# A selective-scan kernel: softplus's last sums moved from matmuls to VectorE for three of four images, and the spread of B issued earlier

## Chip, cores and metric

The kernel runs on one core of one Trainium2 chip. The metric is the device time of one execution in microseconds (us); lower is better. All arithmetic is fp32.

## What is computed

The input is four images of 48 x 48 pixels with 128 channels. Layer 0 is a state-space block with four scan directions; layer 1 is an attention over the pixels followed by a spectral convolution. Cut to what matters here (b image, k direction, d one of 256 inner channels, n one of 16 states, l position):

```python
x_dbl = jnp.einsum('bkdl,kcd->bkcl', xs, x_proj_w)
dts_r, Bs, Cs = x_dbl[:, :, :R], x_dbl[:, :, R:R + N], x_dbl[:, :, R + N:]
dts = jnp.einsum('bkrl,kdr->bkdl', dts_r, dt_proj_w)
dt = jax.nn.softplus(dts + dt_proj_b[None, :, :, None])
A = -jnp.exp(A_logs).reshape(K, d, N)
...
h = h * exp(dt_l * A) + (dt_l * u_l) * B_l      # scanned over l
y = sum over n of h * C_l
...
t = t + attention(layernorm(t))
t = t + spectral_convolution(layernorm(t))
```

The change is in how `dt = softplus(...)` is put together, and in where the spread of B stands in the order of the instructions.

## The kernel before, in words

**Stages.** The images go one after another. For each image there is a prologue (group norm, projections, depthwise convolution), the scans, an epilogue and the attention. The prologue of the next image is woven into the epilogue and the attention of this one. The spectral convolution of image b-1 (`tail`, then `stu`) is woven into the scans of image b; image 0's scans are woven with `mixture`, which makes the convolution's weights G out of the matrices M that it loads. The convolution of the last image runs alone at the end. In the trace the scans of image 0 lie from about 116 to 1202 us, those of images 1, 2 and 3 from about 1470 to 2883, 3149 to 4579 and 4847 to 6256 us.

**Scans.** An image has 24 chunks: four directions of six chunks of 384 positions (`CS`). A chunk has 8 units, one for each half h of the 256 channels and each quarter q of the states. A unit works on a tile s of 128 x 1536. L439 enters it (dt*x times B): on VectorE with B read from PSUM, or, for the three units in `POOLED`, (0, 3), (1, 1) and (1, 3), on GpSimd with B from a tile bc in SBUF. ScalarE makes dA = exp(A*dt) in four pieces (L444), VectorE scans the four pieces (L447), GpSimd copies the carry (L455) and multiplies by C (L456), and TensorE sums over the states (L464). After four units VectorE adds the sum to y (L470).

**Spread of B.** For a unit that VectorE enters, `Unit.spread` (L431) is one matmul that copies B's rows (partitions 32 to 63 of xd) over 128 partitions into a PSUM tile. There is one such tile, so the spread for unit s+2 waits until VectorE has entered unit s+1.

**Preparation of a chunk.** `Chunk.prep` is a generator of 20 steps. Steps 1 to 3 make xd with the matmuls of L354; steps 4 to 7 multiply it with dt's weights, once for each half (L364, rows 0 to 8), and ScalarE takes the absolute value e and the relu of the product (L366, L367). Step 9 is e = exp(-e) and u = 1 + e (L373, L374); step 11 is l = ln(u) and u - 1 (L377, L378). Then softplus is relu + ln(u) with a correction for the rounding of u: e - (u - 1) + l + relu. Four matmuls with an identity (or its negative) for each half make this sum in PSUM (L395); ScalarE copies it to SBUF (L398), and VectorE multiplies it by x (L401). Those are steps 12 and 13 for half 0 and 14 and 15 for half 1. The two results go to DRAM (`store`, L383) and come back replicated as rep (`load`, L388): half 0's store is issued in step 15, half 1's store and half 0's load in step 17, half 1's load in step 19.

**Order of the work.** The order is written out by hand in `scans`; each engine runs its own queue in that order. `prepare` is called twice for each unit, in its middle and at its end, and takes a step of the next chunk in units 0 to 5 of a chunk and of the chunk after in units 4 to 7. So step 11 falls in the middle of a chunk's second unit, step 12 at its end, steps 13 and 14 in the middle and at the end of the third, step 15 in the middle of the fourth. dt's matmuls fall at the ends of the sixth and the seventh unit. `more` takes pieces of the woven work (on images 1 to 3: conv, L945, with its copies on ScalarE, L954, and additions on VectorE, L965; projection, L1003) until a share of all TensorE columns of the stage has been issued; `CHUNK_COLS` counts those of a chunk. Conv has two PSUM tiles. The transfers of rep, bc, tt (the convolution's filters) and G are all issued from SP's queue, in order.

Of the kernel before, what the change touches and what calls it, by code (L numbers as in the profile page):

```python
# [9 lines left out]
AF = mybir.ActivationFunctionType  # L10
ALU = mybir.AluOpType
# [9 lines left out]
NH = D // P  # L21
CS = 384
# [32 lines left out]
def hybrid_kernel(ctx: ExitStack, tc: tile.TileContext, a: dict, out: bass.AP):  # L55
# [3 lines left out]
    nc = tc.nc  # L59
# [60 lines left out]
    spread = wp.tile([64, Q4, C4, DL], F32, name="spread")  # L120
# [6 lines left out]
    mone = wp.tile([P, 1], F32, name="mone")  # L127
# [189 lines left out]
    def in_order(t, k, lo, n):  # L317

        if k % 2 == 0:
            return t[:, lo // W:(lo + n) // W, :]  # L320
        return t.rearrange("p h w -> p w h")[:, lo // H:(lo + n) // H, :]

    def mm_tile(name):
        return psm.tile([P, 512], F32, tag="mm", name=name)

    class Chunk:


        def __init__(self, b, k, c):
            self.b, self.k, self.lo = b, k, c * CS  # L330
            self.name = f"{b}_{k}_{c}"
            self.bc, self.rep = {}, []
            self.rev = k >= 2
            self.first = c == (NCH - 1 if self.rev else 0)
            self.last = c == (0 if self.rev else NCH - 1)

# [6 lines left out]
        def prep(self, pool):  # L343

            k, name, xc = self.k, self.name, xcs[self.b]
            yield
            xd = self.xd = pool.xd.tile([64, CS], F32, tag="xd", name=f"xd{name}")  # L350
            bcd = self.bcd = dram.tile([32, CS], F32, tag="bcd", name=f"bcd{name}")
            ps = mm_tile(f"xp{name}")
            for h in range(NH):
                nc.tensor.matmul(ps[:64, :CS], xw[:, h, k, :], in_order(xc[h], k, self.lo, CS),  # L354
                                 start=(h == 0), stop=(h == NH - 1))
            yield 2 * CS
            nc.scalar.activation(xd, ps[:64, :CS], AF.Identity, bias=onerow)
            yield

            u, l = [pool.one.tile([P, NH, CS], F32, tag=f"tmp{v}", name=f"{v}{name}") for v in "ul"]  # L360
            re = pool.one.tile([P, NH, 2, CS], F32, tag="re", name=f"re{name}")
            for h in range(NH):
                ps = mm_tile(f"dt{name}_{h}")
                nc.tensor.matmul(ps[:, :CS], dtw[:, k, h * P:(h + 1) * P], xd[:R + 1], start=True, stop=True)  # L364
                yield CS
                nc.scalar.activation(re[:, h, 1], ps[:, :CS], AF.Abs)  # L366
                nc.scalar.activation(re[:, h, 0], ps[:, :CS], AF.Relu)  # L367
                if h == 0:
                    nc.sync.dma_start(bcd, xd[32:64])
                yield  # L370
            e = re[:, :, 1]
            yield 0
            nc.scalar.activation(e, e, AF.Exp, scale=-1.0)  # L373
            nc.scalar.activation(u, e, AF.Identity, bias=1.0)  # L374
            yield
            yield 0
            nc.scalar.activation(l, u, AF.Ln)  # L377
            nc.scalar.activation(u, u, AF.Identity, bias=mone)  # L378
            d = dram.tile([NH, DL, 2, G4, CS], F32, tag="dtdu", name=f"dtdud{name}")

            def store(h):
                for g in range(G4):
                    nc.sync.dma_start(d[h, :, :, g], re[g * DL:(g + 1) * DL, h])  # L383

            def load(h):
                rep = pool.rep.tile([P, 2, G4, CS], F32, tag="rep", name=f"rep{name}_{h}")
                for c in range(C4):
                    nc.sync.dma_start(rep[c * DL:(c + 1) * DL], d[h])  # L388
                self.rep.append(rep)

            yield
            for h in range(NH):
                ps = mm_tile(f"sp{name}_{h}")
                for i, (w, t) in enumerate(((ident, e[:, h]), (nident, u[:, h]), (ident, l[:, h]), (ident, re[:, h, 0]))):
                    nc.tensor.matmul(ps[:, :CS], w, t, start=(i == 0), stop=(i == 3))  # L395
                yield 4 * CS

                nc.scalar.copy(re[:, h, 0], ps[:, :CS])  # L398
                x = in_order(xc[h], k, self.lo, CS)
                w = x.shape[2]  # L400
                nc.vector.tensor_tensor(re[:, h, 1].rearrange("p (r w) -> p r w", w=w),  # L401
                                        ps[:, :CS].rearrange("p (r w) -> p r w", w=w), x, ALU.mult)
                if h == 1:
                    store(0)
                yield
            yield 0
            store(1)
            load(0)
            yield
            yield 0  # L410
            load(1)
            yield
# [60 lines left out]
    POOLED = ((0, 3), (1, 1), (1, 3))  # L473
    order = [(k, c) for k in range(K) for c in (range(NCH) if k < 2 else reversed(range(NCH)))]
    quads = [(h, q) for h in range(NH) for q in range(Q4)]
# [1 line left out]
    EARLY = 4  # L477
    FETCHED = sorted({q for h, q in POOLED} | set(range(Q4, 2 * Q4)))

    CHUNK_COLS = (len(quads) - len(POOLED)) * CS + len(quads) * CS + 12 * CS  # L480

    def begin_scans(b, pool):

# [12 lines left out]
    def scans(b, chunks, preps, front, sp, back, work, work_cols):  # L496

        units = [Unit(ch, h, q) for ch in chunks for h, q in quads]
        total = len(chunks) * CHUNK_COLS + work_cols
        done = [0]  # L500

        def more(share):

            while done[0] < share * total:
                cols = next(work, None)
                if cols is None:
                    break
                done[0] += cols

        def enter(s):  # L510

            if s + 2 < len(units) and units[s + 2].pool:
                units[s + 2].enter(sp.s)
            if 0 <= s + 1 < len(units) and not units[s + 1].pool:
                units[s + 1].enter(sp.s)

        def spread(s):
            if s < len(units) and not units[s].pool:
                units[s].spread(back.psB)
                done[0] += CS  # L520

        def prepare(s):

            ci, j = divmod(s, len(quads))
            for c in [ci + 1] * (j <= TURN + 1) + [ci + 2] * (j >= TURN):
                if c < len(chunks):
                    done[0] += next(preps[c], None) or 0

        def refill(s, i):

            if 0 <= s < len(units) and s // len(quads) + 1 < len(chunks):
                u, nxt = units[s], chunks[s // len(quads) + 1]
                if u.h == NH - 1:
                    nxt.fetch(i + u.q, front)

        pending = []
        spread(0)
        enter(-2)
        enter(-1)
        spread(1)  # L540
        for s in range(len(units) + 2):
            real = s < len(units)
            if pending and real:
                pending.pop().add_y()
            enter(s)
            if real:
                units[s].scan(0, back.psa)
            if 1 <= s <= len(units):
                units[s - 1].times_c()
            if real:  # L550
                units[s].scan(1, back.psa)
            prepare(s)
            more((s + 0.5) / len(units))
            spread(s + 2)
            if real:
                units[s].scan(2, back.psa)
                units[s].scan(3, back.psa)
            if pending:
                pending.pop().add_y()
            refill(s - 3, Q4)  # L560
            if s + 1 < len(units) and units[s + 1].pool:
                refill(s + 1, 0)
            if s >= 2:
                units[s - 2].sum_c(back.psy)
                done[0] += CS
                if units[s - 2].q == Q4 - 1:
                    pending.append(units[s - 2])
            more((s + 1) / len(units))
            prepare(s)
        for u in pending:  # L570
            u.add_y()
        assert next(work, None) is None
# [522 lines left out]
    for b in range(B):  # L1095
        sp = Stage(tc, f"h{b}", "left", s=(6, SB))
        ps = Stage(tc, f"b{b}", "right", psa=(2, PSUM), psy=(1, PSUM), psB=(1, PSUM), psc=(2, PSUM), psp=(1, PSUM))
        if b == 0:
            mixed = Stage(tc, "m", "right", two=(2, SB))
            scans(b, *first, front, sp, ps, mixture(mixed, ps), MIX_COLS)  # L1100
            mixed.close()
        else:
            scans(b, *first, front, sp, ps, later(b - 1, held, ps), STU_COLS + TAIL_COLS_ALL)
# [93 lines left out]
```

## Time and profile before

| | us |
|---|---|
| median of 3 runs (lowest, highest) | 7273.59 (7267.72, 7281.86) |
| the profiled execution's own time | 7258.27 |
| its span, first to last instruction | 7256.5 |
| TensorE busy (matmuls) | 6418.8 (88%) |
| VectorE busy | 4834.2 (67%) |
| ScalarE busy | 3020.6 (42%) |
| GpSimd busy | 3809.3 (52%) |
| mean granted TensorE clock | 0.914 |

The shares are means over stages with different limits, so the table of stretches, which gives each engine's busy time between two points of the span, is what a reading rests on. An fp32 matmul stands in the trace as two records. "PEld" is TensorE's loading of weights, which overlaps matmuls. In a wait, "X <- Y" means that X's engine sat idle until Y was done. A few per cent of the matmul records can be missing.

### The profile page before, as it was taken

To read this page: it belongs to the slowest core of one execution; us is meant where nothing else is said; L and a number is where in the kernel's file an instruction comes from. 1 tells how busy PE (TensorE), PEld (TensorE's weight loads), DVE (VectorE), ACT (ScalarE), POOL (GpSimd) and SP (SyncE) were. 2 spreads that over 40 slices of the span, in tenths; PEclk is the share of its full clock that TensorE was granted. 3 is DMA by queue.
4 is the path that set the end of the run, shared out by engine and by line. 5 is a ranking of instruction groups with operands and counts; after the bars stand their busy time and mean duration, and the time that the engine had idled before them with its cause. 6 is when DMAs were issued, how large, how long until landed. Compare 5 with 4: busy or idle time off the path is not lost.

```text
span 7256.5 us, 80192 instructions
## 1 busy us (share of the span) xinstructions
PE 6418.8 (88%) x26904; PEld 3706.4 (51%) x26904; DVE 4834.2 (67%) x6045; ACT 3020.6 (42%) x5984; POOL 3809.3 (52%) x1775
## 2 busy tenths in 40 slices
PE   4777777978999998978999999887999999889999
PEld 1333334434555565534555556533455556647788
DVE  6889986377788876457778886547878887412111
ACT  3666663444444443344444543244444543231000
POOL 2888885056677765035667775215667776300000
PEclk7777777979999999889999999888999999889999
DMA  3555553056667675046667676125667677215545
GB/s 96 137 137 136 133 135 93 22 131 151 166 167 193 174 195 171 14 102 144 157 165 190 179 192 189 47 62 131 166 167 183 184 183 205 78 31 140 152 145 177
DMA packets 648926, 1019.18 MB, mean 140 GB/s; under 512 B 93849, under 2 KB 506649, under 8 KB 623778
## 3 DMA queue, kind: packets, MB, share of 16 engines
q1 hardware_dynamic: 642816, 1010.84, 53.9%
q8 instruction: 214, 3.51, 0.2%
q10 hardware_dynamic: 5698, 3.21, 0.2%
q14 instruction: 198, 1.62, 0.1%
HBM read 895.86 MB, written 117.84 MB: 140 GB/s over the span
## 4 chain that ended last, share of the span: by engine, by line
PE 63%; DVE 20%; DMA 8%; ACT 3%; POOL 2%; issue 2%; SPq 2%; DVEq 0%; ACTq 0%; POOLq 0%
PE cv L945 26%; DVE s L447 11%; PE pr L1003 7%; PE y L464 5%; PE sp L395 5%; DVE s L439 4%; PE s L695 4%; PE B L431 4%; PE o L686 3%; DMA tt<-fd 2%; DMA G<-gd 2%; PE op L632 2%; PE dt L364 2%; PE xp L354 2%; POOL s L456 1%
## 5 line engine op out<-in xcount | busy, mean ns | idle before, releaser
L456 POOL TENSOR_TENSOR s<-s,bc 128x1536 f32<-128x1536 f32 x768 | 2645.0, 3445 | 263.5 <-DVE s L447 187.2
L447 DVE TENSOR_TENSOR_SCAN s<-dA,carry,s 128x384 f32<-128x384 f32 x2560 | 2444.7, 1005 | 311.9 <-ACT dA L444 307.8
L444 ACT ACTIVATE dA<-rep,A 128x384 f32<-128x384 f32 x3072 | 1748.3, 584 | 951.5 <-DVE s L447 935.4
L945 PE MATMUL cv<-tt,u 128*128 128x256 f32 (+4 forms) x7680 | 1682.4, 360 | 83.4 <-DVE U L965 60.3
L945 PEld LDWEIGHTS cv<-tt,u 128*128 128x128 f32 (+1 forms) x7680 | 1282.2, 192 | 652.8 <-issue 298.7
L439 POOL TENSOR_TENSOR s<-rep,bc 128x1536 f32<-128x1536 f32 x288 | 993.8, 3451 | 616.8 <-DMA bc<-bcd 445.6
L965 DVE TENSOR_TENSOR U<-cv,Q 128x256 f32<-128x256 f32 (+1 forms) x1280 | 491.0, 392 | 1078.8 <-PE cv L945 1074.5
L945 PE MATMUL cv<-tt,us 128*128 128x256 f32 (+4 forms) x3840 | 866.3, 361 | 92.6 <-DVE U L965 60.2
L439 DVE TENSOR_TENSOR s<-rep,B 128x1536 f32<-128x1536 f32 x480 | 834.7, 1739 | 83.0 <-PE B L431 72.7
L954 ACT COPY Q<-cv 128x256 f32<-128x256 f32 (+3 forms) x640 | 224.7, 352 | 1576.3 <-PE cv L945 1414.8
L464 PE MATMUL y<-s,csum 128*32 128x384 f32 x6144 | 724.5, 547 | 174.8 <-POOL s L456 157.1
L945 PEld LDWEIGHTS cv<-tt,us 128*128 128x128 f32 (+1 forms) x3840 | 629.2, 190 | 360.9 <-issue 124.7
L1003 PE MATMUL pr<-U,G 128*128 128x512 f32 (+4 forms) x2048 | 729.0, 487 | 65.3 <-DMA G<-gd 60.6
L455 POOL COPY carry<-s 128x4 f32<-128x4 f32 x640 | 122.8, 192 | 1256.1 <-DVE s L447 1168.2
L447 DVE TENSOR_TENSOR_SCAN s<-dA,s 128x384 f32<-128x384 f32 x512 | 457.7, 943 | 66.1 <-ACT dA L444 65.7
L431 PE MATMUL B<-xd,spread 32*128 32x384 f32 x960 | 476.1, 578 | 21.3 <-DVE s L439 20.6
L1003 PEld LDWEIGHTS pr<-U,G 128*128 128x128 f32 x2048 | 339.8, 195 | 285.5 <-issue 191.3
L464 PEld LDWEIGHTS y<-s,csum 128*32 128x32 f32 x6144 | 126.4, 112 | 614.0 <-POOL s L456 309.3
L696 ACT ACTIVATE e<-s,shift 128x512 f32<-128x512 f32 (+1 forms) x360 | 231.9, 644 | 306.0 <-PE s L695 305.0
L395 PE MATMUL sp<-re,ident 128*128 128x384 f32 x768 | 325.2, 506 | 26.1 <-DVE re L401 24.4
L695 PE MATMUL s<-xnT 128*128 128x512 f32 (+1 forms) x720 | 340.2, 556 | 2.1 <-ACT e L696 2.0
L806 PE MATMUL G<-M,W 128*128 128x128 f32 (+2 forms) x768 | 232.8, 452 | 117.9 <-DMA M<-in_M_phi_plus 116.2
(164 smaller groups left out, 4829.1 us busy)
## 6 DMA issues: line engine op xcount, KB each, us to landing
rep<-dtdud SPq DMA_DIRECT2D x768, 384.0 KB, 7.7
tt<-fd SPq DMA_DIRECT2D x192, 577.0 KB, 4.3
bc<-bcd SPq DMA_DIRECT2D x2304, 48.0 KB, 3.8
tt<-fd SPq DMA_DIRECT2D x192, 513.0 KB, 4.1
tt<-fd SPq DMA_DIRECT2D x192, 385.0 KB, 4.0
dtdud<-re SPq DMA_DIRECT2D x768, 96.0 KB, 2.2
G<-gd SPq DMA_DIRECT2D x192, 256.0 KB, 4.3
tt<-fd SPq DMA_DIRECT2D x64, 514.0 KB, 5.3
```

The source lines that it names most:

```text
L395: nc.tensor.matmul(ps[:, :CS], w, t, start=(i == 0), stop=(i == 3))
L431: nc.tensor.matmul(self.bt[:, :CS], spread[32:64, self.q].rearrange("p c j -> p (c j)"), self.ch.xd[32:64], start=True, stop=True)
L439: eng.tensor_tensor(s, self.ch.rep[self.h][:, 1], bt.unsqueeze(1).to_broadcast([P, G4, CS]), ALU.mult)
L444: nc.scalar.activation(dA[:, :CS], ch.rep[self.h][:, 0, g], AF.Exp, scale=A[:, ch.k, self.h * G4 + g, self.q:self.q + 1])
L447: nc.vector.tensor_tensor_scan(s, dA[:, CS - 1::-1] if ch.rev else dA[:, :CS], s, 0.0 if ch.first else carry[:, self.h, self.q, g:g + 1], ...
L456: nc.gpsimd.tensor_tensor(self.s, self.s, ch.bc[Q4 + self.q].unsqueeze(1).to_broadcast([P, G4, CS]), ALU.mult)
L464: nc.tensor.matmul(ch.y[g * DL:(g + 1) * DL, :CS], csum, self.s[:, g], start=(self.q == 0), stop=(self.q == Q4 - 1))
L695: nc.tensor.matmul(p[:, :w], xnT[:, i * P:(i + 1) * P], xnT[:, lo:lo + w], start=True, stop=True)
L806: nc.tensor.matmul(p[:, :n] if j else p[:, NF - 1 - i], W[:, q if t else 0, i], M[t][:, i].unsqueeze(1).to_broadcast([P, n, C]) if j else ...
L945: nc.tensor.matmul(p2[:, :, at - first:], x, t[:kp, :, hi - 1 - at + J * P:end if end >= 0 else None:-1], start=(J == 0), stop=(J == nb - 1))
L965: nc.vector.tensor_tensor(dst, src, q, ALU.add)
L1003: nc.tensor.matmul(p[:, :, :v], Gs[n][:, q, x, :], U[n][:, 4 * q:4 * q + 4, :v], start=False, stop=(k == KF - 1 and q == 1 and v == w))
```

## The change

For images 1 to 3 (`on_vector`), ScalarE no longer subtracts 1 from u, and the matmuls of L395, ScalarE's copies and VectorE's products from PSUM are not issued. In their place VectorE works on both halves at once in SBUF: u = (u - 1) - e in step 12, l = l - u in step 13, relu = relu + l in step 14, and the two products by x in step 15, which also issues half 0's store, as before. The number of steps stays 20. The count of columns for a chunk loses the 8 x 384 of those matmuls for images 1 to 3. For all images, the spread of B for unit s+2 is issued straight after the step of the preparation in the middle of unit s, before the woven work instead of after it.

```diff
+            self.on_vector = b > 0
...
             nc.scalar.activation(l, u, AF.Ln)
-            nc.scalar.activation(u, u, AF.Identity, bias=mone)
+            if not self.on_vector:
+                nc.scalar.activation(u, u, AF.Identity, bias=mone)
...
-            for h in range(NH):
+            if self.on_vector:
+
+                nc.vector.scalar_tensor_tensor(u, u, -1.0, e, ALU.add, ALU.subtract)
+                yield 0
+                nc.vector.tensor_tensor(l, l, u, ALU.subtract)
+                yield
+                nc.vector.tensor_tensor(re[:, :, 0], re[:, :, 0], l, ALU.add)
+                yield 0
+                for h in range(NH):
+                    x = in_order(xc[h], k, self.lo, CS)
+                    w = x.shape[2]
+                    dt, dx = [re[:, h, i].rearrange("p (r w) -> p r w", w=w) for i in range(2)]
+                    nc.vector.tensor_tensor(dx, dt, x, ALU.mult)
+                store(0)
+                yield
+            for h in range(0 if self.on_vector else NH):
                 ps = mm_tile(f"sp{name}_{h}")
...
-    CHUNK_COLS = (len(quads) - len(POOLED)) * CS + len(quads) * CS + 12 * CS
+    def chunk_cols(b):
+
+        return (len(quads) - len(POOLED)) * CS + len(quads) * CS + (4 if b else 12) * CS
...
-        total = len(chunks) * CHUNK_COLS + work_cols
+        total = len(chunks) * chunk_cols(b) + work_cols
...
             prepare(s)
+            spread(s + 2)
             more((s + 0.5) / len(units))
-            spread(s + 2)
```

## The prediction

> **What bounds the kernel now.** I read the page first, then the table of stretches (us, then busy time of PE, PEld, DVE, ACT, POOL with instruction counts, granted clock, DMA share, GB/s), then waits and single stretches in order of time. The slices show DVE full in image 0's scans (slices 2 to 7) and PE full in those of images 1 to 3.
>
> ```profile
> PE   4777777978999998978999999887999999889999
> DVE  6889986377788876457778886547878887412111
> PEclk7777777979999999889999999888999999889999
> ```
>
> A chunk (8 units) runs from one dt*x product (L401) to the next chunk's. Two chunks of image 0, then four of image 2:
>
> ```profile
> 597.58:638.04 40.46, 33.63 (x135) 13.91 (x134) 40.41 (x41) 26.10 (x46) 34.91 (x17) 0.79 0.59 138
> 638.04:683.96 45.92, 33.27 (x134) 13.78 (x134) 39.38 (x42) 28.31 (x54) 37.55 (x14) 0.70 0.57 133
> ...
> 3563.00:3631.20 68.20, 61.07 (x232) 31.83 (x231) 45.76 (x58) 27.15 (x54) 39.59 (x20) 0.90 0.59 138
> ...
> 4117.80:4169.30 51.50, 51.50 (x224) 29.55 (x224) 43.35 (x50) 25.70 (x49) 38.23 (x18) 1.00 0.69 180
> 4222.90:4274.40 51.50, 51.50 (x223) 29.31 (x223) 43.08 (x49) 25.77 (x50) 36.84 (x19) 1.00 0.71 180
> ...
> 4328.80:4392.00 63.20, 61.70 (x356) 40.60 (x354) 45.14 (x57) 25.49 (x51) 40.93 (x20) 1.00 0.73 203
> ```
>
> Image 0: a chunk lasts as long as VectorE is busy (40.41 of 40.46), or 6 us longer where a transfer of M is late. Image 2's middle: PE is busy 51.50 of 51.50. Three groups in image 2: S, 12 chunks from 3694.6 to 4328.8: 52.9 us each, PE 51.7, DVE 44.3. E, 7 chunks from 3251.7: 63.3, PE 56.5, DVE 47.0; PE waits for U and G, and runs at a lower clock. L, 2 chunks from 4328.8: 67.2, PE 64.7, DVE 45.1. The waits of image 2's scans (total, times, longest) say the same: VectorE and ScalarE wait for PE more than PE waits for VectorE.
>
> ```profile
> DVE U L965 <- PE cv L945: 164.8, 144, 13.8
> DVE s L447 <- ACT dA L444: 113.6, 89, 8.2
> ACT re L398 <- PE sp L395: 107.5, 44, 4.3
> ...
> PEld cv L945 <- DVE U L965: 75.4, 77, 3.5
> ```
>
> **What the Trainium skill says.** "SBUF — State Buffer", section "SBUF: two separate sides": VectorE's second SBUF port is GpSimd's port, locked for a whole instruction; a VectorE instruction with two SBUF inputs and a GpSimd one exclude each other. The trace agrees:
>
> ```profile
> 1528.26 1.73 DVE L163 TENSOR_TENSOR u<-u,ln_vu 64x512 f32<-64x512 f32 x1
> ```
> ```profile
> 1526.02 3.42 POOL L439 TENSOR_TENSOR s<-rep,bc 128x1536 f32<-128x1536 f32 x1
> 1529.38 0.65 POOL L455 COPY carry<-s 128x4 f32<-128x4 f32 x1
> ```
>
> That product takes 0.67 alone; it ended 1529.99, just after GpSimd's 1529.44, and the carry copy behind it took 0.65, not 0.19: they take turns. "TensorE: Matmul & The Clock Gate", Part 3: matmuls on different row groups run at once. It agrees: dt's product (rows 0 up) and B's spread (rows 32 up) cost one where they are neighbours:
>
> ```profile
> 1530.71 1.00 PE L364 MATMUL dt<-xd,dtw 9*128 9x384 f32 x1
> 1530.72 1.00 PE L431 MATMUL B<-xd,spread 32*128 32x384 f32 x1
> 1531.51 0.84 PE L364 MATMUL dt<-xd,dtw 9*128 9x384 f32 x1
> 1531.52 0.84 PE L431 MATMUL B<-xd,spread 32*128 32x384 f32 x1
> ```
>
> Same page, Part 1: idling halves the clock. It agrees: after 3.31 us of waiting for G at 3597.56 a dt pair took 1.64, against 0.91 at 3587.51.
>
> **The change, part by part, per chunk of images 1 to 3.**
>
> *Removed from PE:* 8 fp32 matmuls (16 records) on L395. In S they are busy 65.82/12 = 5.5 us; 5.5 in E and L too.
>
> *Moved:* the spread of B (one matmul with its weights, no transfer) ahead of the conv work. In the changed order 177 of 192 dt products have a spread right behind them (4 before); a spread hidden saves 0.84, two per chunk, so about 1.5. It is also ready sooner: image 0 lost 45.3 us to VectorE waiting for B (9 times), images 1 to 3 23.0. Against it: the spread needs the PSUM tile that VectorE's L439 frees, and conv queued behind it now waits too. For image 0 I take a quarter of 45.3, -11; bounds +10 and -35.
>
> *ScalarE:* off go the subtraction (0.94) and two copies (0.48 each), 1.9 us, and with the copies its waits for PE, behind which dA stood. I count nothing: in S ScalarE is busy 25.8 of 52.9. If VectorE becomes the bound this is what keeps dA early.
>
> *Added to VectorE:* one scalar_tensor_tensor and two tensor_tensor of 128x768. L279, the same size with two SBUF inputs, takes 0.958, about 0.88 from start to start: 2.65 together. The two dt*x now read SBUF instead of PSUM: still 0.56 or 0.82, nothing.
>
> *Waits for the port* are in no row of such instructions here; bounds 0 and 11.5 (3.65, 4.45 and 3.45, every turn lost; below nothing is excluded, since a lock gives no time). By the queue: the first (end of the chunk's second unit) starts right behind the unit's last scan; GpSimd is idle there (3741.1 to 3744.3), wait 0. GpSimd's carry and product with C (3.64) start behind it. The second comes after an addition (0.8) and two scans (1.9): about 1.0 is left to wait. Then GpSimd's L439 for (1,1), ready, takes its turn (3.44), while VectorE does two scans (1.9): the third waits 1.4. The dt*x pair stands behind L439 (1.7) and two scans, when GpSimd is just done: 0. Sum 2.4. Queued behind each: the scans and the U additions, for which PE's two conv tiles wait.
>
> *SP:* the store of half 0 keeps its place in the queue, but its data now come with half 1's, one unit later. SP stands at stores already (103.3 us in S); G, tt and bc fetches between the stores wait that unit. I take no cost in the likeliest case, as tt has four buffers; it is a rival below. GpSimd gains nothing and waits some 3 us behind VectorE, with 52.9 - 38.8 to spare.
>
> *Sum.* S: PE 51.7 - 5.5 - 1.5 = 44.7; DVE 44.3 + 2.65 + 2.4 = 49.4. So VectorE becomes the end, and I add 1.8 for units in which it still waits: 51.2, that is -1.7 x 12 = -20. E: PE's 7.0 saved, of which I give back 2.5 as later U additions: -4.5 x 7 = -31. L: PE still ends, DVE 50: -6.5 x 2 = -13. The ragged first and last chunks, and the first chunk's sums under attention: -4. Together -68 per image, x 3 = -204; with image 0's -11, -215. The profiled execution took 7258.3 (span 7256.5), so 7043; the median of the runs, 7273.6, lies 15.3 above it: **7058**.
>
> **Rivals.**
> *PE's whole saving arrives* (the port costs nothing, B early keeps VectorE fed): S falls to 47.9 (-5.0 x 12), E -7 x 7, L -7 x 2, the rest -5: -128 per image, image 0 -30: 6860. More likely it arrives for the greater part, 6920. For: VectorE can run at 40.41 of 40.46. Against: GpSimd is busy 73% of S. Chance 0.12.
> *Transfers late:* 3.3 items per chunk fetch G, so 0.4 of the chunks have one in the unit between the stores. If one chunk in four then stalls PE by 3 us and pays 5 more at half clock, 24 x 0.25 x 8 = 48 per image: 7202. For: E chunks already wait for G. Against: in S no wait for G. Chance 0.19.
> *VectorE loses its turns* (slower): GpSimd's product with C gets in ahead of the first addition (3.65) and between the two dt*x (3.45), or its next instruction ahead of the second (+2.05). The place is the second to fourth unit of a chunk. A us of wait costs about 19 us an image (S and E), and 72 an image are to be lost, so it decides from 2.4 + 3.8 = 6.2 us of waiting per chunk. With 8: +34 per image, 7365. For: carry and first addition wait for the same scan. Against: the turn taken at 1529.4. Chance 0.14.
>
> **How the numbers follow.** Likeliest 0.55, its own range 6970 to 7170. Leaving out half of the first rival and most of the last, the range is 6940 to 7270. A measurement of this kernel tells apart about 0.2% (15 us). Faster: 0.55 + 0.12 + 0.13 of the late transfers; same 0.04; slower 0.14 + 0.02.
>
> **What would show it.** In the profile after: no matmuls into sp; 128x768 rows on VectorE with a mean of 0.96 plus 0.5 to 1.1; S chunks at about 51 with VectorE busy 49 and PE 45; pairs of dt and B at equal starts; image 0's waits for B below 45. Wrong if the 128x768 rows mean over 2.5 us, if PE waits for G or tt grow, or if PE's clock falls below 0.95 in S.

## The result and the profile after

The changed kernel takes 7593.72 us in the median of 4 runs (7580.9 to 7601.09), the kernel before on the same chip 7274.18: a ratio of 1.0437, 95% interval 1.0417 to 1.0457. It is 320 us slower; 7058 had been forecast. The profiled execution's span is 7584.9 us. From the page's first two parts:

```profile
PE 6261.6 (83%) x25752; PEld 3571.8 (47%) x25752; DVE 5229.1 (69%) x6261; ACT 2909.6 (38%) x5768; POOL 3919.2 (52%) x1775
...
PE   4777777967888898967888898877888898889999
...
DVE  6888886477888976467788886547788987612111
...
PEclk7777776978999988878899998887898998899999
```

The 1152 records of the removed matmuls are gone (25752 for 26904). At the clock of S they were worth 5.5 us a chunk, 396 us in 72 chunks, but TensorE is busy only 157 us less: of the 25 slices with a granted clock of 9 before, 9 stand at 7 or 8 now (mean over the span 0.864 for 0.914), and the remaining matmuls last longer. VectorE is busy 395 us more. The chain that ended last has turned from 63% PE, 20% DVE and 8% DMA to this (a q marks an engine's sequencer):

```profile
PE 48%; DVE 25%; DMA 13%; issue 4%; POOL 4%; ACT 3%; SPq 3%; DVEq 0%; ACTq 0%; POOLq 0%
```

By stage, a stage of scans ending where the epilogue's first matmul starts: the scans of image 0 end at 1246.2 us, 44 us later than before (1201.9); images 1 to 3 take 100, 79 and 105 us more each, from one image's end of scans to the next (3027.4, 4802.1 and 6585.0, before 2882.9, 4578.8 and 6256.3). The table of stretches for image 2, chunk by chunk (from the first addition of one chunk to that of the next: us, then busy PE, PEld, DVE, ACT, POOL, the clock, DMA share, GB/s); one early chunk, two of the middle, one late:

```profile
3535.33:3603.55 68.22, 53.76 (x193) 25.41 (x195) 52.71 (x62) 25.88 (x51) 40.44 (x19) 0.83 0.61 149
...
4103.73:4159.67 55.94, 48.02 (x216) 27.66 (x215) 49.33 (x58) 25.67 (x48) 40.49 (x20) 0.94 0.69 176
4267.29:4317.08 49.79, 46.73 (x214) 26.46 (x212) 47.84 (x56) 24.24 (x45) 40.65 (x19) 1.00 0.68 171
...
4610.08:4680.96 70.88, 64.41 (x340) 42.70 (x339) 50.31 (x61) 24.06 (x48) 39.03 (x20) 0.83 0.66 181
```

Twelve chunks in the middle (3739.5 to 4425.6) last 57.2 us on average, with VectorE busy 49.7 and PE 49.4. Of the chunks shown, only the third, in which PE keeps its full clock, comes near what was forecast (51.2, with VectorE at 49.4 and PE at 44.7). In the changed kernel the line numbers have moved: L464 is the scan, L456 the enter, L473 the product with C, L472 the carry, L461 dA, L448 the spread, L481 the sum over the states, L964 the conv and L984 its additions. The rows of the new instructions by form:

```profile
L396 DVE SCALAR_TENSOR_TENSOR u<-u,re 128x768 f32<-128x768 f32 x72 | 166.4, 2311 | 46.2 <-ACT l L378 46.2
...
L400 DVE TENSOR_TENSOR re<-re,l 128x768 f32<-128x768 f32 x72 | 135.4, 1880 | 0.1
...
L398 DVE TENSOR_TENSOR l<-l,u 128x768 f32<-128x768 f32 x72 | 127.5, 1771 | 0.1
...
L406 DVE TENSOR_TENSOR re<-re,xc 128x384 f32<-128x384 f32 x144 | 92.8, 683 | 0.1
```

L396, L398 and L400, called the additions from here on, last 2.31, 1.77 and 1.88 us in the mean instead of some 0.93 (measured below without a wait). And in the waits of the whole span (total, times, longest) TensorE now stands for VectorE in two places, the conv's additions U and the tile of B. Before, the four PE lines, in the order of this list, were 220.4, 120.5, 20.6 and 44.8 us:

```profile
PEld cv L964 <- DVE U L984: 510.8, 266, 7.8
DVE s L464 <- ACT dA L461: 485.6, 299, 11.2
PE cv L964 <- DVE U L984: 377.8, 146, 7.4
...
PE B L448 <- DVE s L456: 171.7, 124, 7.4
PEld B L448 <- DVE s L456: 157.8, 112, 8.6
```

One chunk of image 2 in order of time shows how these hang together (start, duration, instruction; in brackets the idle time before it):

```profile
4102.76 0.59 PE L964 MATMUL cv<-tt,u 128*128 128x256 f32 x2
4102.85 0.19 POOL L472 COPY carry<-s 128x4 f32<-128x4 f32 x1 [2.54 <-DVE s L464]
...
4103.12 3.44 POOL L473 TENSOR_TENSOR s<-s,bc 128x1536 f32<-128x1536 f32 x1
...
4103.39 0.42 DVE L984 TENSOR_TENSOR U<-cv,Q 128x256 f32<-128x256 f32 x1 [0.60 <-PE cv L964]
4103.73 3.64 DVE L396 SCALAR_TENSOR_TENSOR u<-u,re 128x768 f32<-128x768 f32 x1
...
4106.51 4.18 POOL L456 TENSOR_TENSOR s<-rep,bc 128x1536 f32<-128x1536 f32 x1
...
4109.74 1.76 DVE L398 TENSOR_TENSOR l<-l,u 128x768 f32<-128x768 f32 x1
...
4118.44 0.74 DVE L984 TENSOR_TENSOR U<-cv,Q 128x256 f32<-128x256 f32 x2
...
4118.90 1.22 PE L964 MATMUL cv<-tt,u 128*128 128x256 f32 x2 [5.12 <-DVE U L984]
```

Between the unit's last scan and the first addition stands a U addition, which waits for PE. GpSimd's carry and product with C need only the scan, so they start first; the addition issued at 4103.73 ends at 4107.37, 0.81 us after GpSimd's product. The next one ends at 4111.50, 0.81 us after GpSimd's L456. It is so throughout: of the 216 additions 141 last over 1.3 us, and each of these ends 0.81 to 0.82 us after a GpSimd instruction that ended while it stood. The U addition whose matmuls were done at 4112.99 comes up at 4118.44, behind the third addition, an enter, two scans and the products. PE has idled 5.12 us by then, and its next two matmul records take 1.22 us where two of the same form took 0.59 at 4102.76: twice as long.

### The profile page after: what moved, and what is told of

Its sections match the earlier page's. It is cut to its first block, busy times and chain, and to the rows that moved or that the text cites. A ratio compares the mean times of both kernels' runs of the same rounds, so it can differ in the third digit from the quotient of the medians.

```text
span 7584.9 us, 77738 instructions
## 1 busy us (share of the span) xinstructions
PE 6261.6 (83%) x25752; PEld 3571.8 (47%) x25752; DVE 5229.1 (69%) x6261; ACT 2909.6 (38%) x5768; POOL 3919.2 (52%) x1775
## 4 chain that ended last, share of the span: by engine, by line
PE 48%; DVE 25%; DMA 13%; issue 4%; POOL 4%; ACT 3%; SPq 3%; DVEq 0%; ACTq 0%; POOLq 0%
PE cv L964 20%; DVE s L464 10%; DVE s L456 5%; PE pr L1022 5%; DMA rep<-dtdud 5%; PE y L481 4%; PE s L714 4%; PE o L705 3%; DMA tt<-fd 3%; POOL s L473 3%; PE B L448 2%; DMA G<-gd 2%; PE op L651 2%; PE G L825 2%; DVE u L396 2%
## 5 line engine op out<-in xcount | busy, mean ns | idle before, releaser
L473 POOL TENSOR_TENSOR s<-s,bc 128x1536 f32<-128x1536 f32 x768 | 2661.9, 3467 | 309.0 <-DVE s L464 239.2
L464 DVE TENSOR_TENSOR_SCAN s<-dA,carry,s 128x384 f32<-128x384 f32 x2560 | 2437.8, 999 | 414.0 <-ACT dA L461 412.6
L461 ACT ACTIVATE dA<-rep,A 128x384 f32<-128x384 f32 x3072 | 1758.7, 584 | 1463.5 <-DVE s L464 1411.0
L964 PE MATMUL cv<-tt,u 128*128 128x256 f32 (+4 forms) x7680 | 1792.1, 375 | 322.1 <-DVE U L984 318.1
L964 PEld LDWEIGHTS cv<-tt,u 128*128 128x128 f32 (+1 forms) x7680 | 1327.4, 199 | 980.1 <-DVE U L984 400.2
L456 POOL TENSOR_TENSOR s<-rep,bc 128x1536 f32<-128x1536 f32 x288 | 1040.6, 3613 | 632.1 <-DMA bc<-bcd 622.1
L984 DVE TENSOR_TENSOR U<-cv,Q 128x256 f32<-128x256 f32 (+1 forms) x1280 | 488.6, 390 | 1067.8 <-PE cv L964 1064.2
L964 PE MATMUL cv<-tt,us 128*128 128x256 f32 (+4 forms) x3840 | 941.0, 383 | 107.1 <-DVE U L984 59.7
L481 PE MATMUL y<-s,csum 128*32 128x384 f32 x6144 | 797.5, 597 | 236.0 <-POOL s L473 189.7
L472 POOL COPY carry<-s 128x4 f32<-128x4 f32 x640 | 166.0, 259 | 1406.0 <-DVE s L464 1361.7
L964 PEld LDWEIGHTS cv<-tt,us 128*128 128x128 f32 (+1 forms) x3840 | 676.5, 205 | 425.4 <-issue 190.6
L1022 PE MATMUL pr<-U,G 128*128 128x512 f32 (+4 forms) x2048 | 768.1, 505 | 98.3 <-DMA G<-gd 78.8
L456 DVE TENSOR_TENSOR s<-rep,B 128x1536 f32<-128x1536 f32 x480 | 832.8, 1735 | 16.9 <-DMA rep<-dtdud 11.3
L448 PE MATMUL B<-xd,spread 32*128 32x384 f32 x960 | 501.9, 606 | 173.0 <-DVE s L456 171.7
L464 DVE TENSOR_TENSOR_SCAN s<-dA,s 128x384 f32<-128x384 f32 x512 | 456.9, 937 | 73.3 <-ACT dA L461 73.0
L481 PEld LDWEIGHTS y<-s,csum 128*32 128x32 f32 x6144 | 132.0, 117 | 643.2 <-POOL s L473 303.5
L705 PE MATMUL o<-e,xn 128*128 128x512 f32 (+1 forms) x720 | 333.7, 549 | 0.0
L448 PEld LDWEIGHTS B<-xd,spread 32*128 32x128 f32 x960 | 158.5, 205 | 350.7 <-DVE s L456 157.8
```

Source lines behind the costliest of these rows:

```text
L448: nc.tensor.matmul(self.bt[:, :CS], spread[32:64, self.q].rearrange("p c j -> p (c j)"), self.ch.xd[32:64], start=True, stop=True)
L456: eng.tensor_tensor(s, self.ch.rep[self.h][:, 1], bt.unsqueeze(1).to_broadcast([P, G4, CS]), ALU.mult)
L461: nc.scalar.activation(dA[:, :CS], ch.rep[self.h][:, 0, g], AF.Exp, scale=A[:, ch.k, self.h * G4 + g, self.q:self.q + 1])
L464: nc.vector.tensor_tensor_scan(s, dA[:, CS - 1::-1] if ch.rev else dA[:, :CS], s, 0.0 if ch.first else carry[:, self.h, self.q, g:g + 1], ...
L473: nc.gpsimd.tensor_tensor(self.s, self.s, ch.bc[Q4 + self.q].unsqueeze(1).to_broadcast([P, G4, CS]), ALU.mult)
L481: nc.tensor.matmul(ch.y[g * DL:(g + 1) * DL, :CS], csum, self.s[:, g], start=(self.q == 0), stop=(self.q == Q4 - 1))
```

## The experiments

Each kernel ran beside the kernel before on its chip; ratios are to that, with 95% intervals, and 0.1% is 7.3 us. Interval ends lie 0.15 to 0.3% from the ratio, so differences below some 20 us say nothing.

**One part alone.** The sums on VectorE with the spread in its old place:

```diff
             prepare(s)
-            spread(s + 2)
             more((s + 0.5) / len(units))
+            spread(s + 2)
```

> Only the sums are moved to VectorE; the spread of B stays behind the woven work, as in the kernel before. Theory A (the moved spread does the harm: PE stands at it while VectorE is late, and the conv work queued behind it is late too): about 7100, the saving that was forecast. Theory B (VectorE's burst of three additions and two products in the second to fourth unit of a chunk, with its waits for GpSimd's port, starves PE of U additions for about 5 us and halves its clock; the spread costs only what image 0 lost, 44 us): about 7540. Both alike: about 7420.

Measured: 7512.39 us, 1.0308 (1.0292 to 1.0323), 228 us slower than before. The spread moved alone, the sums left on PE:

> Only the spread of B is moved, for all four images; the sums stay on TensorE. Theory A: 44 us lost in each image, and more in images 1 to 3: 7450 to 7590. Theory B: about 7318 (image 0's 44 us, and little in images 1 to 3, where PE ends everything and 1.5 us per chunk of dt and B at once may give up to 100 back: down to 7220).

Measured: 7390.69 us, 1.0142 (1.0123 to 1.0161), 107 us slower. Added up the two give 4.5%, the whole change 4.37%: within the noise the parts cost independently of each other. The spread moved alone shows its mechanism in image 0 (this is its trace):

```profile
871.92 1.64 PE L431 MATMUL B<-xd,spread 32*128 32x384 f32 x2 [1.58 <-DVE s L439]
...
873.49 2.08 PE L806 MATMUL G<-M,W 128*128 128x256 f32 x4
...
876.94 2.55 PE L806 MATMUL G<-M,W 128*128 128x128 f32 x16
...
878.19 0.48 ACT L811 COPY Gm<-G 128x384 f32<-128x384 f32 x1 [3.87 <-PE G L806]
...
878.56 1.09 ACT L444 ACTIVATE dA<-rep,A 128x384 f32<-128x384 f32 x2
...
879.19 1.93 DVE L447 TENSOR_TENSOR_SCAN s<-dA,carry,s 128x384 f32<-128x384 f32 x2 [2.02 <-ACT dA L444]
```

The spread stands at the head of PE's queue until VectorE has entered the unit before; G's matmuls come late behind it; ScalarE's copy of G waits 3.87 us for them; behind the copy stands dA; and VectorE's scan waits 2.02 us. It comes again: image 0's waits of the copy for G rise from 37.0 us (14 times) to 89.8 (24 times) and those of the scans for dA from 38.9 to 121.1, while VectorE's waits for B fall from 45.3 to 1.7. Image 0 ends 45 us later. Images 1 to 3 lose 39, 13 and 41 us; there PE's waits at B's tile have grown (over the whole span 159.6 and 157.5 us for 20.6 and 44.8), but their way to the end was not followed.

Is the spread a gain at least right behind dt's product, where matmuls on two row groups can run at once? The spread moved only in the last two units of a chunk:

```diff
+            beside = s % len(quads) >= TURN + 2
+            if beside:
+                spread(s + 2)
             more((s + 0.5) / len(units))
-            spread(s + 2)
+            if not beside:
+                spread(s + 2)
```

> The kernel before with the spread moved ahead of the woven work only in the seventh and eighth unit of a chunk, where dt's product stands right in front of it; elsewhere it stays behind. If dt and B at once are worth what they cost alone (0.84 us twice a chunk, 72 chunks in which PE ends): about 7160. If standing at the spread costs as much there as it saves: 7270, no change.

Measured: 7307.5 us, 1.0033 (1.0017 to 1.005). PE is busy 53 us less (6365.7), but nothing of it reaches the end; the waits at B's tile (20.6 and 44.8 us before, 58.9 and 60.3 now) have grown meanwhile. And only half of the pairs run at once: of the 190 dt products in the trace 177 now have a spread right behind them, as was forecast for the changed order, but in only 96 do the two start within 0.03 us of each other; the other spreads start up to 3.1 us later. In the changed kernel it is 93 of 177.

**The port.** The kernel with the sums alone, its three additions taking one operand from PSUM (the product with dt's weights) instead of two from SBUF:

```diff
+                pp = ps[:, :CS].unsqueeze(1).to_broadcast([P, NH, CS])
-                nc.vector.scalar_tensor_tensor(u, u, -1.0, e, ALU.add, ALU.subtract)
+                nc.vector.scalar_tensor_tensor(u, u, -1.0, pp, ALU.add, ALU.min)
-                nc.vector.tensor_tensor(l, l, u, ALU.subtract)
+                nc.vector.tensor_tensor(l, l, pp, ALU.min)
-                nc.vector.tensor_tensor(re[:, :, 0], re[:, :, 0], l, ALU.add)
+                nc.vector.tensor_tensor(re[:, :, 0], re[:, :, 0], pp, ALU.max)
```

> The kernel with only the sums moved, but the second operand of the three 128x768 instructions is the product with dt's weights in PSUM in place of a tile in SBUF, and they take minima and a maximum, so that dt is the relu alone: one SBUF input, no port to share. Same count and size of instructions. Theory B with the port as the main part of it: the mean of the three falls from about 2.0 to 1.1 us and the time falls by 150 to 220 us against the kernel with the sums only. If the burst itself (2.9 us of work) does it and not the port: within 60 us of it.

Measured: 7327.32 us, 1.0057 (1.0041 to 1.0074): 185 us below the same kernel with both operands in SBUF, on the same chip. Its rows by form, where those of the sums alone have means of 2324, 1785 and 1622 ns:

```profile
L407 DVE TENSOR_TENSOR re<-re,xc 128x384 f32<-128x384 f32 x144 | 109.8, 802 | 0.1
...
L397 DVE SCALAR_TENSOR_TENSOR u<-u,dt 128x768 f32<-128x768 f32 x72 | 67.7, 940 | 46.2 <-ACT l L378 46.2
L401 DVE TENSOR_TENSOR re<-re,dt 128x768 f32<-128x768 f32 x72 | 67.2, 934 | 0.1
...
L399 DVE TENSOR_TENSOR l<-l,dt 128x768 f32<-128x768 f32 x72 | 66.8, 927 | 0.0
```

So 2.80 us a chunk is their own run and 2.93 us, 211 us in all, is waiting for the port. The products behind them, with two operands in SBUF as ever, take back 17 us of it (802 ns each for 684), so that VectorE is busy 191 us less in all (5016.5 for 5207.4), which is worth 185 us of time. One addition only, the other two and so the correction left out:

> The kernel with only the sums moved, without the first two of VectorE's three additions (dt is relu plus ln(u); the correction for the rounding of 1 + e is left out). The port theory: of 4.9 us of additions and waits per chunk some 1.9 to 2.9 are left at one place, so about two thirds of what the port cost come back: 7320 to 7390. If it is the burst's work and not the port, the remaining addition is a third of it: 7300 or less.

Measured: 7307.68 us, 1.0045 (1.0022 to 1.0068). The one addition (L398 there) lasts 2284 ns in the mean: it takes over the wait that the first of three had. No addition at all, dt being the relu alone:

> The kernel of the sums alone (spread in its old place, 7512 us) with all three VectorE instructions left out: in images 1 to 3 dt is the relu alone, everything else, ScalarE's work, the products, the stores, stays. If the three instructions carry the whole of the sums' price, by their own run (127 us by the sums from PSUM) and by the port (185 us), it comes to about 7200, as the softplus on ScalarE does with the same products (7200). If ScalarE's longer chain (absolute value, relu, two more passes) carries a part, it lands between 7230 and 7320, near the kernel with one addition (7308).

Measured: 7198.66 us, 0.9907 (0.9882 to 0.9932). From here, one addition costs 1.4% (100 us), three without the port 1.5% (109 us), the port's waits another 2.5%. The first two must not be set against the length of the additions (164 and 202 us), since the port is waited for all the same where they are left out, by the products:

```profile
L403 DVE TENSOR_TENSOR re<-re,xc 128x384 f32<-128x384 f32 x144 | 163.5, 1175 | 42.0 <-ACT u L375 42.0
```

With one addition the products take 732 ns each, with three from PSUM 802, with three from SBUF 684. In its whole busy time VectorE has 97 us more with one addition (4984.6 for 4887.8) and 129 more with three from PSUM (5016.5). And the kernel without additions equals the next one, whose ScalarE does less (2755.1 us for 2913.6): that part of ScalarE's work carries nothing of the loss that can be told.

**PE's saving by itself.** For images 1 to 3 softplus is one Ln(Exp + 1) on ScalarE, with no sums on any engine, the products as in the changed kernel, the spread in its old place:

```diff
+                    nc.scalar.activation(re[:, h, 1], ps[:, :CS], AF.Exp)
...
+                nc.scalar.activation(re[:, :, 0], e, AF.Ln, bias=1.0)
```

> For images 1 to 3 dt is ln(1 + exp(x)) in two steps of ScalarE: no sums on TensorE and none on VectorE, only the two products by x; the absolute value, the relu and the correction are left out, the spread stays behind the woven work. If TensorE's 5.5 us per chunk are worth their length where nothing else is late: 7020 to 7110. If in these stages the time is set by the coupling of VectorE and TensorE and not by TensorE's own work: 7230 to 7280.

Measured: 7200.09 us, 0.9896 (0.987 to 0.9923). The same with the eight matmuls issued for nobody:

> As e9_softplus_on_scalar, but the eight matmuls per chunk are issued again, with no reader, where they stood before. Its distance from e9 is what TensorE's 5.5 us per chunk are worth: 150 to 250 us if TensorE's work ends the chunks, under 50 if not. Its distance from the kernel before is what ScalarE's copies, standing ahead of dA, were worth: 7250 to 7280 if nothing.

Measured: 7461.26 us, 1.0253 (1.0233 to 1.0273). That is 260 us above the kernel without them, but also 185 above the kernel before, which has as many matmuls and more work on ScalarE: so another thing was in it. Both have the two products in one step, and the store of half 0 behind them. With half 0's product one unit earlier, as before the change:

```diff
-                yield 0
-                yield
-                yield 0
-                for h in range(NH):
+                def product(h):
...
+                yield 0
+                product(0)
+                yield
+                yield 0
+                product(1)
                 store(0)
```

> The kernel with the softplus on ScalarE alone and no sums (7200 us), with one edit: the product of half 0 with x is issued one unit earlier, in the step in which the kernel before has it; half 1 and the stores stay where they are. As in that kernel, the absolute value, the relu and the correction are left out in images 1 to 3, so dt is another sum of the same quantities there. If the store of half 0, which now waits for a product issued just ahead of it, holds up SyncE's queue and with it G, dt|du and the other loads (the theory), the time falls by 100 to 185 us, to 7015 to 7100. If the late store is hidden, it stays within 20 us of 7200, and the rest of what PE should have saved went elsewhere.

> The kernel with the softplus on ScalarE and the eight matmuls a chunk issued without a reader (7461 us), with the product of half 0 one unit earlier as in the kernel before; the same parts left out. It has the matmuls of the kernel before, less ScalarE work and both products from SBUF. If the late store is what makes it 185 us slower than before, it falls to 7250 to 7300. If the port at the products is the cause, or the unread matmuls themselves, it stays above 7400.

Measured: 7184.7 us without the matmuls, 0.9872 (0.9855 to 0.9889), which tells nothing from 0.9896: the expected gain is missing. With them 7304.57 us, 1.0039 (1.0024 to 1.0055), 2.1% or 157 us less than with both products late. Both differences are net of something else: half 0's early product waits for GpSimd, so VectorE is busy 55 and 75 us more with it (the products last 1596 ns in the mean for 1222 without the matmuls, 1550 for 1048 with them). A late half 0 is dear where PE has the matmuls; where it hasn't, what it costs and what it saves seem to balance. What the eight matmuls cost depends on it too: 260 us with half 0 late, 7304.57 - 7184.7 = 120 us with it early, where VectorE's busy time is the same on both sides (4950.0 and 4949.9). So of 396 us of PE's time 66% or 30% arrives, never all of it. For the second pair the waits say where the rest stays; first the kernel with the matmuls, then the one without:

```profile
PEld cv L977 <- DVE U L997: 254.0, 232, 3.5
...
PE cv L977 <- DVE U L997: 155.0, 138, 3.1
```
```profile
PEld cv L970 <- DVE U L990: 422.1, 289, 5.5
...
PE cv L970 <- DVE U L990: 295.3, 170, 5.1
```

The same conv matmuls wait for the same U additions, only longer, up to 5.5 us, and the clock falls from 0.908 to 0.895. Spread moved in the kernel without sums, to see whether its price depends on them:

> As e9_softplus_on_scalar, with the spread of B moved for all images as in the changed kernel. If standing at the spread costs whatever else is going on: about 107 us more than e9. If it costs only because TensorE has no time to lose: 44 us more (image 0) or a little over.

Measured: 7318.47 us, 1.0042 (1.0022 to 1.0063), 118 us above; as dear as beside PE's sums (107).

**The products and the late store, in the kernel before.** The products read ScalarE's copy of dt in SBUF instead of PSUM, steps unchanged; then also both in one step, the store behind them:

```diff
-                nc.vector.tensor_tensor(re[:, h, 1].rearrange("p (r w) -> p r w", w=w),
-                                        ps[:, :CS].rearrange("p (r w) -> p r w", w=w), x, ALU.mult)
+                dt, dx = [re[:, h, i].rearrange("p (r w) -> p r w", w=w) for i in range(2)]
+                nc.vector.tensor_tensor(dx, dt, x, ALU.mult)
```

> The kernel before with one edit in all images: the two products a chunk read dt from its copy in SBUF and no longer from the sum in PSUM; steps unchanged. The sums stay on PE. If GpSimd's port is dear at the products (1 to 2 us of waiting each, and a wait for ScalarE's copy), 30 to 120 us over before, 7305 to 7395; if the products are short enough to slip in, within 20 us of before, 7255 to 7295.

> The kernel of the products from SBUF with one edit more: the product of half 0 stands right ahead of that of half 1, one unit later than before, and the store of half 0 right behind both, as in the changed kernel; all images. If the late store costs what the theory says, this is 100 to 185 us slower than the same kernel with half 0 in its old step; if the late store is hidden, within 20 us of it.

Measured: 7475.32 us, 1.0265 (1.0246 to 1.0284), and 7534.3 us, 1.0354 (1.0328 to 1.038). The first was expected at 120 us more at the most and costs 200. The products' row, before and in this run:

```profile
L401 DVE TENSOR_TENSOR re<-sp,xc 128x384 f32<-128x384 f32 x192 | 130.7, 680 | 194.6 <-ACT re L398 194.2
```
```profile
L402 DVE TENSOR_TENSOR re<-re,xc 128x384 f32<-128x384 f32 x192 | 330.6, 1722 | 182.8 <-ACT re L398 182.8
```

The wait in front of them is not new. New is their length, 200 us in all, and VectorE's whole busy time grows by 193 us (5027.3 for 4834.2): about as much as the kernel loses. In images 1 to 3 alone it is 147 us more of busy time and 167 us more of time, in the stages of which the middle had counted as PE's.

The late store adds 59 us over four images, less than expected, but again this is a net figure: the late products wait less (1057 ns), VectorE is busy 130 us less, and the kernel is slower all the same. What the late store costs by itself is therefore likely more than 59 us; no run shows it alone. Its way is visible: SP's waits for the products rise from 990.1 to 1162.7 us, and PE's for G from 45.9 and 37.4 to 107.9 and 84.2.

**Products on GpSimd.** One word of the softplus on ScalarE with half 0 early: `nc.gpsimd.tensor_tensor(dx, dt, x, ALU.mult)`.

> The softplus on ScalarE with half 0 early (7185 us; the same parts left out), with the two products of a chunk of images 1 to 3 on GpSimd instead of VectorE, in the same steps. VectorE loses 230 us of such instructions, of which some 130 are waits for the port. If the port at the products costs what it costs at the additions, 60 to 130 us faster, 7055 to 7125; if GpSimd's own queue (its products with C and B stand ahead) makes the stores late, 7185 or slower.

Measured: 7007.35 us, 0.9641 (0.9618 to 0.9663), the fastest kernel of this study, and 177 us below the same with the products on VectorE, where they took 229.5 us with their waits (1596 ns each); VectorE is busy 207 us less (4743.2 for 4949.9). In image 0 too, with the products on VectorE and on GpSimd:

> The softplus on ScalarE with half 0 early (7185 us), done in image 0 too, whose scans are bound by VectorE; absolute value, relu and correction are left out in all images, so dt is another sum of the same quantities. If image 0's products pay for the port as those of images 1 to 3 do (0.9 us each, 48 of them on the engine that ends there), it is 20 to 50 us slower, 7205 to 7235; if PE's and ScalarE's relief reaches VectorE there, 7140 to 7180.

> The softplus on ScalarE and the products on GpSimd (7007 us) in image 0 too; absolute value, relu and correction are left out in all images, so dt is another sum of the same quantities. VectorE ends image 0's scans, and loses 48 products of 0.67 us there, 32 us: 6965 to 6995 if that reaches the end; above 7000 if GpSimd, busiest in image 0, makes the stores late.

Measured: 7204.27 us, 0.9922 (0.9894 to 0.995), and 7041.69 us, 0.9685 (0.9658 to 0.9711): 20 and 34 us slower (0.50 and 0.44% by the ratios), so image 0 is better left alone. With the products on VectorE, those of image 0 last 1862 ns each, so they wait for GpSimd there too. With them on GpSimd the end of image 0's scans moves from 1204.0 to 1241.3 us although VectorE is busy less (922 for 953 us): its waits for B grow from 46.8 to 108.0. I had expected the relief to reach the end. The products on GpSimd with PE's sums, and with the additions on VectorE:

> The kernel before with one edit in all images: the two products a chunk are issued on GpSimd and read dt from ScalarE's copy; sums stay on PE, spread in its old place. If the products are what VectorE can best do without (no wait for PE's sums in front of the scans, 128 us of run time), 7100 to 7200; if ScalarE's copy is what the products wait for in any case and the stores come late, 7250 to 7330.

> The kernel of the sums alone (additions on VectorE, spread in its old place, 7512 us) with the products on GpSimd. The three additions stay on VectorE and keep their waits for the port. If the port's price at the products adds to that at the additions, 7512 less 100 to 180, 7330 to 7410; if the additions take over the waits (GpSimd is busier then), above 7450.

Measured: 7403.33 us, 1.0179 (1.0156 to 1.0202), a miss, and its cause stays open. GpSimd stands 613.1 us at ScalarE's copy, but some 500 of that is one long wait ahead of each image's scans, which the fastest kernel has as well (410.7 us in three waits); in the scans themselves it is some 113 us in 76 waits. PE's waits for G have grown too (97.1 and 77.5 us for 60.6 and 43.4), and of the 127 us that the kernel loses 47 are image 0's. And 7478.31 us, 1.0275 (1.0249 to 1.0302), only 34 us below the sums alone (0.3% by the ratios): the products had few waits there to lose (684 ns each), and the additions keep theirs (2524, 1784, 1627 ns).

## Why the prediction was wrong, by its own steps

**What bounds the kernel: the failed step.** The prediction read "PE is busy 51.50 of 51.50" as PE being the end of a chunk, and took every us that comes off PE (7.0 a chunk, 5.5 of them the matmuls) for a us off the chunk until VectorE's busy time is reached. VectorE's new 5 us a chunk were charged in full only in S, with 2.5 us in E and with nothing in L. The runs give the rates, by time divided by the engine's busy time, over the whole kernel:

| | time / busy time, us | rate |
|---|---|---|
| PE's eight matmuls, half 0 early | 120 / 396 | 0.30 |
| the same, half 0 late | 260 / 396 | 0.66 |
| VectorE: products from SBUF in the kernel before | 200 / 193 | 1.0 |
| VectorE: one addition | 100 / 97 | 1.0 |
| VectorE: three additions from PSUM | 109 / 129 | 0.85 |
| VectorE: the port's waits at the additions | 185 / 191 | 0.97 |
| VectorE: products taken off it | 177 / 207 | 0.86 |

So a us on VectorE cost nearly a us already in the kernel before, though it was the less busy engine, and one taken off PE gave back a third to two thirds. Even with no addition on any engine, which leaves of the sums' change only what it removes and the moved products, the kernel is 0.9% or some 70 us faster, where the forecast had 215 us for the whole change with its additions. The likely reason is argued, from the waits: PE's conv and VectorE's U additions pass work to and fro through two PSUM tiles, and VectorE's queue is in order, so the softplus matmuls stood for a good part where PE would have waited for U anyway.

**The sum of S.** VectorE's load came out almost as worked out: 49.7 us in the middle chunks for 49.4. What failed is "I add 1.8 for units in which it still waits: 51.2". The chunk is 57.2, so 7.5 us of waiting remain. The 1.8 came from image 0, where VectorE runs at 40.41 of 40.46 with no conv beside it; in image 2 it shares the loop with PE. For PE 44.7 was forecast and the trace has 49.4: about as many matmul records as the 12 chunks of S had after the removal (2540 for 2758 - 192) ran at a clock of 0.93 instead of 1.00. In E, -4.5 us a chunk was forecast; five chunks from 3389.4 to 3739.5 now last 70.0 in the mean, where E had 63.3.

**Waits for the port.** The sum, 2.4 us, came out as 3.16 in the changed kernel (2311 + 1880 + 1771 less 2801 ns). Its largest error is the first addition: 0 was said, since it "starts right behind the unit's last scan"; it waits 1.37 us in the mean, because U additions stand between. The second and third wait 0.84 and 0.95 (1.0 and 1.4 said), the products hardly, as said (683 ns for 680 before). The Trainium skill ("SBUF — State Buffer", section "SBUF: two separate sides") states the exclusion of two-input VectorE instructions and GpSimd's; the runs agree and add the control, 0.93 us each as soon as one operand is in PSUM. The rate, "19 us an image" for a us of waiting, was nearly right: that would be 167 us for the 2.93 us of the sums alone, and 185 was measured.

**The spread.** Counted as a gain of 1.5 us a chunk and 11 us in image 0; it lost 107 us, of which 45 in image 0, outside the bounds of +10 and -35 set there. The hidden spread was mis-sized: 177 spreads stand right behind a dt product, as said, but only half of them start with it. The prediction named the wait ("conv queued behind it now waits too") and didn't price it. Nor did it follow the queue on to G, to ScalarE's copy and to dA, which in image 0 lie on VectorE's path.

**The late store.** Counted as nothing. In the three pairs of runs with half 0 early and late, late was 15 (too little to tell), 59 and 157 us slower while VectorE was busy 55, 130 and 75 us less. By the rates above that should have saved time, so the late store very likely has a price of its own. No run moved half 0 in the changed kernel itself, so its share there stays open. PE's waits for G did grow, from 60.6 and 43.4 us to 78.8 and 89.3.

**ScalarE.** Counting nothing agrees with the runs (no additions 0.9907, softplus on ScalarE 0.9896).

**The signs of being wrong.** Of the three that were set, two came: PE's waits for G grew, and PE's clock in the middle chunks is 0.93. The third didn't: the three rows of 128x768 have a mean of 1.99 us, in the range that was expected.

**The rivals.** That PE's whole saving arrives is ruled out by its rates. Late transfers were named, and the waits for G and for the stores agree with them, but their share in the changed kernel was not isolated. The slower end came about in part by the mechanism named for it, VectorE losing turns to GpSimd, but at half of the 6.2 us that were said to be needed: the gain against which it was weighed wasn't there. In per cent of the kernel before, the steps lie thus: all removals with the products moved and late, -0.9; the three additions without waits, +1.5 (less than their length, because the products lose waits); the port, +2.5; the spread, +1.3; together +4.4.

## What to carry to other kernels

Busy all the time is not the same as setting the end: two engines that hand work to each other through a few buffers share the path, and a us may be dearer on the one that is less busy. Before work is moved from the busier to the less busy engine, ask what stands behind it in that queue and who waits for it, and measure one us on each side. Count an engine's busy time as a whole: a wait that leaves one instruction may turn up at the next. Put VectorE's new work where one operand is in PSUM or where GpSimd idles; and don't move an instruction that must wait ahead of work that needn't.

## What the runs showed of the hardware that was not expected

- A two-input SBUF instruction of VectorE beside a GpSimd engine that is busy 71% of the time (the twelve middle chunks) lasted 1.6 to 2.3 us in the mean for 0.93, and one alone (2284 ns) waited as long as the first of three (2324): the wait belongs to the place and not to the number, and where the additions were left out the products behind them waited (1175 ns for 684).
- The price of a short idle stretch on TensorE: after 5.12 us of waiting, two records took 1.22 us for 0.59. The Trainium skill ("TensorE: Matmul & The Clock Gate", Part 1) says that idling halves the clock, and this agrees. With it goes that PE is busy only 157 us less for 396 us removed; how much of the difference is the clock's was not measured apart.
- In image 0, whose scans VectorE bounds, moving the products to GpSimd ended the scans later, by 37 us with softplus on ScalarE and by 47 us with the sums on PE (1249.2 for 1201.9), though VectorE was busy some 30 and 25 us less. As PE kept its matmuls in the second, less work for PE is not the common cause; which wait it is was not isolated.
